# A two-layer graph net on one core: all projections in pairs of seven half products, y first, then layer 0

## The chip, the core and the metric

The kernel runs on one core of one Trainium2 chip. The time of a run is the device time in microseconds; lower is better. The core has five engines with an instruction queue each: TensorE (PE, matmuls; its weight loads are listed as PEld), VectorE (DVE), ScalarE (ACT), GpSimd (POOL) and SyncE (SP, which here only issues DMAs). Each engine works through its own queue in the order that was fixed when the program was built, and waits on semaphores of the others.

## What is computed

There are N = 2708 rows of D = 1024 float32 numbers and an adjacency matrix of zeros and ones with 10,979 ones. The reference, cut to what matters:

```python
# layer 0
q = x @ W_q.T + b_q;  k = x @ W_k.T + b_k;  v = x @ W_v.T + b_v
z = (q @ k.T) / sqrt(1024) * adj
z = where(z == 0, -10000, z)
x1 = layernorm(x + relu(softmax(z, axis=1) @ v))
# layer 1
out = layernorm(x1 + adj @ (x1 @ weight) + bias)
```

A row without neighbours has only masked scores, so its softmax is even over all rows and its layer-0 sum is the mean of all rows of v. 178 rows are of this kind.

## The kernel before

The kernel uses that the matrix is sparse. Rows are sorted by their number of neighbours and cut into 22 blocks of 128 (the last has 20 rows). `SLOTS` gives for each block how many neighbours its rows may have; block 0 holds the rows with most neighbours and is treated in shares, "hub" among them. Blocks 0 to 7 are the first family, 8 to 21 the second. A flag, computed on the chip, sends inputs that don't fit to a dense fallback, which this input doesn't use.

The score of rows i and j is x_i M x_j plus a term in j and i alone, with M = Wq^T Wk. So the kernel works in these stages:

- **0 to 138 us.** The weights are loaded and turned, M is made (L627, 256 matmuls, copied by ScalarE into `m_sb`), and VectorE and ScalarE look for the ones of the adjacency matrix, one block of columns at a time (`list_columns`, L235).
- **y, 138 to about 520 us.** `y_block` makes y = xM + bias for a block: 16 matmuls of 128 rows against 512 columns (L336), two accumulators, two additions by VectorE into one of two buffers `yo` (L340), and a store to y_d in DRAM. `column_sums` adds the columns of x on ScalarE meanwhile (L349), and `load_x` fetches a later block of x^T into one of three buffers. The 14 y blocks of the second family are woven together with the attention of the first.
- **Layer 0.** For each block GpSimd gathers the rows of y (L360) and the neighbours' rows of x (L366) by indirect DMA, VectorE forms the scores (L831) and, after the softmax, the weighted sum r (L888, L965). Then r is turned by TensorE (16 transposes, L734) and copied by ScalarE (L735), multiplied by Wv^T, finished on VectorE (bias, relu, residual) and ScalarE (layer norm), and scattered to x1_d (L721).
- **Layer 1, from about 747 us.** The neighbours' x1 rows are gathered and added (L1256, L1259), turned, multiplied by w1, normed and scattered to the output, in "units" of two blocks; the first unit is block 20 alone.

The product by Wv exists in two forms. `project` does one block in 16 matmuls (L757): blocks 6, 5, 4, 3, 2, 1, 0 take it, as "v" steps between y blocks or behind them. `pair_products` does two blocks at once. It cuts both turned blocks and the weight into halves, and takes seven half products of four matmuls (L1017) in place of eight. For that it needs four sums S of the turned halves (`turn_pair`, L1006 to L1009, VectorE) and differences of the weight's quarters (made once, L1154 and its neighbours), and each accumulator is read by VectorE more than once (`add`, L1029): seven reads for a pair. Seven pairs of layer 0, and ten units of layer 1, take this form. `project_mean` handles the last block, all of whose rows have the same sum.

The order is made by a planner at build time. `steps` is a list of products in order: y blocks, "v" steps, then pairs. `jobs` is a list of attention pieces. Each step adds a credit of TensorE time (`STEP`, 14.7, or twice that for a pair), each job takes its estimated VectorE time off (`SLOT`, `SMALL`), and jobs are emitted while credit is left and while fewer sums r are alive than there are buffers (`RB`). A scheduler then orders each queue; evictions have a high priority (`URGENT`).

```python
for h in range(NH):
    po = p_o.tile([P, HALF], F32, name="po")
    for c in range(DC):
        put = nc.tensor.matmul(po, xt[:, c, :], m_sb[c // 2][:, c % 2, k0:k1], ...)
    nc.vector.tensor_add(yo[:n, k0:k1], po[:n], y_bc[:n, k0:k1])
```

Of the kernel before, what the change touches and what calls it, by code (L numbers as in the profile page):

```python
# [31 lines left out]
SLOTS = [15, 11, 8, 6, 5, 4, 3, 2] + [13, 5, 4, 4, 3, 3, 3, 2, 2, 2, 1, 1, 1, 0]  # L32
ALONE = [8]
# [5 lines left out]
EARLY = 15  # L39
G1 = 9  # L40
RB = 3
# [39 lines left out]
def sparse_part(ctx, tc, x, xT, adj, wqT, wkT, wvT, bq, bk, bv, w1, b1, out):  # L81
# [29 lines left out]
    with es:  # L111
# [88 lines left out]
        loaded, sorted_, products, applied = [], [], [], []  # L200
# [88 lines left out]
        def load_x():  # L289
            b = len(xts)  # L290
            if b == NB:
                return
            r0, n = b * P, rows[b]
            xt = xa.tile([P, DC, P], F32, name="xt", bufs=3)
            if n < P:
                nc.gpsimd.memset(xt, 0.0)
            nc.sync.dma_start(out=xt[:, :, :n], in_=xT[:, r0:r0 + n].rearrange("(c p) n -> p c n", p=P))
            xts.append(xt)

        load_adj()  # L300
        load_x()
        load_x()
        load_x()
        yos = [xa.tile([P, YW], F32, name=f"yo{k}", bufs=1) for k in range(2)]
        def y_block(b):
            r0, n = b * P, rows[b]
            xt = xts[b]
            if b == NB - 1:
                column_sums(b)

                nc.vector.tensor_reduce(xbT, xs, AX.X, ALU.add)
                nc.vector.tensor_scalar_mul(xbT, xbT, 1.0 / N)
            yo = yos[b % 2]
            y_d, o0 = y_ds[b >= FAMILY], r0 - FAMILY * P * (b >= FAMILY)
            if b == NB - 1:

                assert n <= HUB
                po = p_o.tile([P, HALF], F32, name="po")
                with tc.high_priority(URGENT):
                    for c in range(DC):  # L320
                        for g in range(G):
                            nc.tensor.matmul(po[g * HUB:(g + 1) * HUB, :YW // G], xt[:, c, :HUB],
                                             m_sb[c // 2][:, c % 2, g * YW // G:(g + 1) * YW // G], start=(c == 0), stop=(c == DC - 1))
                    for g in range(G):
                        gs, cs = slice(g * HUB, g * HUB + n), slice(g * YW // G, (g + 1) * YW // G)
                        nc.vector.tensor_add(yo[gs, cs], po[gs, :YW // G], y_bc[gs, cs])
                for g in range(G):
                    gs, cs = slice(g * HUB, g * HUB + n), slice(g * YW // G, (g + 1) * YW // G)
                    nc.sync.dma_start(out=y_d[o0:o0 + n, cs], in_=yo[gs, cs])
                return  # L330
            firsts = []
            for h in range(NH):
                k0, k1 = h * HALF, (h + 1) * HALF
                po = p_o.tile([P, HALF], F32, name="po")
                for c in range(DC):
                    put = nc.tensor.matmul(po, xt[:, c, :], m_sb[c // 2][:, c % 2, k0:k1], start=(c == 0), stop=(c == DC - 1))  # L336
                    if c % (DC // 2) == 0:
                        firsts.append(put)
                with tc.high_priority(URGENT):
                    nc.vector.tensor_add(yo[:n, k0:k1], po[:n], y_bc[:n, k0:k1])  # L340
            products.append(put)
            if b < NB - 1:
                column_sums(b, firsts)
            load_x()
            nc.sync.dma_start(out=y_d[o0:o0 + n, :D], in_=yo[:n, :D])
# [257 lines left out]
        def records_back(f, behind=None):  # L603
            b0, nb = families[f]
            bs, js = slice(b0, b0 + nb), slice(0, max(SLOTS[max(b0, 1):b0 + nb]))
            if f == 0:
                deg0 = lists.tile([P, 1], F32, name="deg0")
                follow(nc.vector.tensor_copy(deg0, tab0[:, DEG:DEG + 1]), products[-1])
                nc.vector.tensor_scalar_add(deg0[:HUB], deg0[:HUB], float(-J0))
                masks(valid0, less0, deg0)  # L610
# [6 lines left out]
        m_sb = [wm_pool.tile([P, 2, YW], F32, name=f"m_sb{q}", tag=f"m{q}") for q in range(4)]  # L617
        for q in range(4):
            nc.vector.memset(m_sb[q][:, :, D:], 0.0)
            nc.vector.tensor_copy(m_sb[q][:, :, D], u_col[:, 2 * q:2 * q + 2])  # L620
        done = 0
        for i in range(DC):
            for h in range(NH):
# [5 lines left out]
                nc.scalar.copy(m_sb[i // 2][:, i % 2, hs], po)  # L629
# [5 lines left out]
                if not sorted_ and done > FAMILY + 2:  # L635
                    sort_end(0)
                    sorted_.append(0)
        y_bc = xa.tile([P, YW], F32, name="y_bc", bufs=1)
# [10 lines left out]
        for b in range(FAMILY):  # L649
            while done < min(NB, EARLY + 2 * (b + 1)):  # L650
                list_columns()
                done += 1
            y_block(b)
            if b in (0, 1, 3, 4, 5, 6):
                next(deal)
            if b == FAMILY - DC // 2 - 3:
                wv_q = quarters_of("wv")
            elif FAMILY - DC // 2 - 2 <= b < FAMILY - 2:
                for c in range(2 * (b - FAMILY + DC // 2 + 2), 2 * (b - FAMILY + DC // 2 + 2) + 2):
                    for h in range(NH):  # L660
                        put = nc.sync.dma_start(out=wv_q[c // 4][h][:, c % 4, :],
                                                in_=wvT[c * P:(c + 1) * P, h * HALF:(h + 1) * HALF])
                        follow(put, products[-2])
            if b == FAMILY - 4:
                sort_begin(1)
            if b == FAMILY - 3:
                sort_end(1)
            if b == 0:
                records_back(0)
# [23 lines left out]
        c_all = stat.tile([P, NB - 1, YW - D], F32, name="c_all", bufs=1)  # L693
        nc.vector.memset(c_all, 0.0)
        def row_constants(f):
            b0, end = families[f][0], min(sum(families[f]), NB - 1)
            for b in range(b0, end):
                xg = g_tile()
                nc.sync.dma_start(out=xg, in_=x[b * P:(b + 1) * P])
                nc.vector.scalar_tensor_tensor(junkv, xg, 1.0, u_bc, op0=ALU.mult, op1=ALU.mult, accum_out=c_all[:, b, 0:1])  # L700
            put = nc.vector.tensor_scalar(c_all[:, b0:end, 0], c_all[:, b0:end, 0], y_bc[:, D:D + 1], None, op0=ALU.add)
            nc.sync.dma_start(out=y_ds[f][:(end - b0) * P, D:].rearrange("(b p) e -> p b e", p=P), in_=c_all[:, b0:end])
            return put

        put = row_constants(0)
        records_back(1, put)

# [3 lines left out]
        def gather_x(src, b):  # L711

            xr = wp.tile([P, D], F32, name="xr", bufs=3)
# [38 lines left out]
        def project(rT, w):  # L752
            po = []
            for h in range(NH):
                acc = p_o.tile([P, HALF], F32, name="po")
                for c in range(DC):
                    put = nc.tensor.matmul(acc, rT[:, c, :], w[c // 4][h][:, c % 4, :],  # L757
                                           start=(c == 0), stop=(c == DC - 1))
                po.append(acc)
            products.append(put)  # L760
            return po

        def project_mean(rT, w):

            acc = p_o.tile([P, HALF], F32, name="po")
            with tc.high_priority(URGENT):
                for c in range(DC):
                    for g in range(G):
                        k = g % 2 * D // G
                        nc.tensor.matmul(acc[g * HUB:(g + 1) * HUB, :D // G], rT[:, c, :],  # L770
                                         w[c // 4][g // 2][:, c % 4, k:k + D // G], start=(c == 0), stop=(c == DC - 1))
# [3 lines left out]
            for h in range(NH):  # L775
                acc = p_o.tile([P, HALF], F32, name="po")
                for g in range(h * G // NH, (h + 1) * G // NH):
                    k = g * D // G - h * HALF
                    put = nc.tensor.matmul(acc[:HUB, k:k + D // G], ident[:, g * HUB:(g + 1) * HUB], quarters,
# [65 lines left out]
        def attend(b, got):  # L845
# [4 lines left out]
            for i, (j0, j1) in enumerate(cut):  # L850
# [33 lines left out]
                else:  # L884
                    r = xb_pools[0].tile([P, D], F32, name="r") if b in ALONE else wp.tile([P, D], F32, name="r", bufs=RB)
# [7 lines left out]

        def mean_rows(b):
# [4 lines left out]
            r = wp.tile([P, D], F32, name="r", bufs=RB)  # L899
# [18 lines left out]
        def finish0(b, po, xr):  # L918
            n = rows[b]
            t = xb_pools[0].tile([P, D], F32, name="t", bufs=3) if b in [0] + last else wp.tile([P, D], F32, name="t")  # L920
# [10 lines left out]
        def attend_shares(b, got):  # L931
# [4 lines left out]
            else:  # L936
                J, tab, far_less, rec, to, far, top = J0, tab0, less0, tab0, to_0, far_0, top2[:, 1:2]
                r = wp.tile([P, D], F32, name="r", bufs=RB)
# [56 lines left out]
        def turn_pair(flips, pool):  # L995

            A = []
            for k, flip_to in enumerate(flips):
                rT = (pool if k else wp).tile([P, DC, P], F32, name="rT", bufs=2)
                A.append(flip_to(rT))  # L1000
            if len(flips) == 1:
                return A, None
# [3 lines left out]
            nc.vector.tensor_add(S[0], a21, a22)  # L1006
            nc.vector.tensor_sub(S[1], S[0], a11)
            nc.vector.tensor_sub(S[2], a11, a21)
            halves_turned.append(nc.vector.tensor_sub(S[3], a12, S[1]))  # L1009
# [5 lines left out]
        def half_products(acc, a, w, start=True, stop=True):  # L1015
            for k in range(DC // 2):
                put = nc.tensor.matmul(acc, a[:, k], w[:, k], start=start and k == 0, stop=stop and k == DC // 2 - 1,  # L1017
# [644 lines left out]
```

## Time and profile before

| | |
|---|---|
| median of three runs | 1067.79 us (1062.9 to 1069.05) |
| the profiled execution | 1068.97 us, its span on the core 1067.1 us |
| mean granted TensorE clock | 0.983 |
| DMA | 229.25 MB, mean 215 GB/s |
| L757, single products by Wv | 97.8 us in 224 records |
| L734, transposes | 43.0 us in 320 records |
| L627, product M | 110.5 us in 256 matmuls, 40 to 138 us |

The times in the page are from one profiled execution. "Busy" is the time in which an engine works on an instruction that isn't a wait, a branch or a DMA issue. A group's row gives the line, the engine, what is written and read with their shapes, the count of records, their busy time and mean duration, and then the idle time just before them with the instruction that ended most of it. A float32 matmul leaves two records. Of the chain of waits that ended last, TensorE holds 23% of the span in the part that could be followed back:

```profile
PE 23%; DVE 11%; issue 6%; DMA 5%; POOL 4%; ACT 1%; POOLq 0%; DVEq 0%
```

The first y block starts in a gap: TensorE begins it at 138.40, stands still for 4.08 us until ScalarE has copied a part of the bias row `y_bc`, and goes on at 145.30. VectorE is then still busy with column lists, and comes to the first addition of y at 159.41.

### The profile page before, as it was taken

Reading aid. Unit: us, or ns where it says so; the run is one execution under the profiler, and the core shown is the slowest. Engines: PE = TensorE matmul, PEld = TensorE weight load, DVE = VectorE, ACT = ScalarE, POOL = GpSimd, SP = SyncE. Lnnn points to the kernel's source line nnn. Section 1 sums busy time; section 2 is a strip of 40 time slices with the busy share of each in tenths; the row PEclk is TensorE's granted clock in tenths of the full one; section 3 lists DMA queues with packets and bytes.
Section 4 is the critical chain, followed back from the end, with each engine's and each line's share of the span. In section 5 each row is a group of like instructions: output and inputs, shape, how many; then the busy total and the mean of one; then the engine's idle time right before and its main releaser. Section 6 shows DMA issues by size and latency. Waiting matters only on the chain.

```text
span 1067.1 us, 10904 instructions
## 1 busy us (share of the span) xinstructions
PE 1007.6 (94%) x2849; PEld 475.4 (45%) x2849; DVE 813.5 (76%) x2021; ACT 426.5 (40%) x894; POOL 494.0 (46%) x534
## 2 busy tenths in 40 slices
PE   7999989999998999999999999999589999999993
PEld 6444444444443444444544444444334444454441
DVE  8999789435387879999399999965677876987432
ACT  4599994222032332224424344332323363333321
POOL 0000350046454445526157666511677777887300
PEclk9999999999999999999999999999789999999997
DMA  9688867534777656796443778726689589979701
GB/s 349 214 285 255 254 184 256 160 116 119 269 262 234 223 172 207 224 346 192 162 127 94 243 241 267 253 80 229 162 278 264 179 276 318 293 210 321 191 40 42
DMA packets 106288, 229.25 MB, mean 215 GB/s; under 512 B 22898, under 2 KB 50298, under 8 KB 106216
## 3 DMA queue, kind: packets, MB, share of 16 engines
q0 software_dynamic: 48768, 148.05, 43.8%
q1 hardware_dynamic: 57448, 80.42, 23.3%
q8 instruction: 24, 0.39, 0.1%
q14 instruction: 48, 0.39, 0.1%
HBM read 219.61 MB, written 33.68 MB: 237 GB/s over the span
## 4 chain that ended last, share of the span: by engine, by line
PE 23%; DVE 11%; issue 6%; DMA 5%; POOL 4%; ACT 1%; POOLq 0%; DVEq 0%
PE po L1017 20%; DMA g<-x_d,tabs 3%; DVE r L888 3%; DVE junkv L831 2%; POOL g L366 1%; PE po L757 1%; DVE t L1029 1%; POOL xr L360 1%; DMA yg<-y_d,tabs 1%; PE tr L734 1%; DVE r L1259 1%; PE tr L747 1%; ACT junks L793 1%; DVE t L1087 1%; POOL r L366 0%
## 5 line engine op out<-in xcount | busy, mean ns | idle before, releaser
L336 PE MATMUL po<-m_sb,xt 128*128 128x512 f32 x672 | 293.7, 596 | 5.5 <-DVE yo L340 5.5
L336 PEld LDWEIGHTS po<-m_sb,xt 128*128 128x128 f32 x672 | 127.0, 191 | 163.4 <-issue 153.4
L831 DVE SCALAR_TENSOR_TENSOR junkv<-yg,g 128x1024 uint8<-128x1024 f32 x109 | 132.8, 1219 | 41.2 <-DMA yg<-y_d,tabs 20.0
L366 POOL DMA_INDIRECT g<-in_x_dram,tabs x86 | 112.1, 1304 | 70.6 <-DVE r L888 21.1
L1017 PE MATMUL po<-t,s_all 128*128 128x512 f32 x272 | 125.9, 606 | 4.7 <-DVE xr L1029 4.7
L1259 DVE SCALAR_TENSOR_TENSOR r<-g,valid,r 128x1024 f32<-128x1024 f32 x77 | 98.6, 1281 | 19.5 <-DMA g<-x_d,tabs 18.8
L627 PE MATMUL po<-wk_o,wq_o 128*128 128x512 f32 x256 | 110.5, 592 | 0.0
L757 PE MATMUL po<-wv,rT 128*128 128x512 f32 x224 | 97.8, 594 | 2.6 <-ACT junka L349 2.1
L793 ACT ACTIVATE junks<-t,lnm 128x1024 uint8<-128x1024 f32 (+1 forms) x41 | 47.0, 1147 | 125.6 <-DVE lnm L791 95.4
L349 ACT ACTIVATE junka<-xt 128x128 f32<-128x128 f32 x176 | 54.1, 307 | 91.9 <-PE po L336 69.6
L366 POOL DMA_INDIRECT g<-x_d,tabs x67 | 79.5, 1186 | 22.7 <-issue 14.0
L1017 PE MATMUL po<-w,rT 128*128 128x512 f32 x192 | 86.4, 599 | 0.0
L888 DVE SCALAR_TENSOR_TENSOR r<-g,pr,r 128x1024 f32<-128x1024 f32 x64 | 81.8, 1279 | 5.2 <-ACT r L900 4.6
L1017 PEld LDWEIGHTS po<-t,s_all 128*128 128x128 f32 x272 | 52.3, 194 | 71.8 <-issue 61.7
L235 DVE FIND_INDEX8 at_a<-ones,a 128x8 uint16<-128x83 f32 (+3 forms) x132 | 82.5, 631 | 0.6 <-issue 0.6
L806 ACT ACTIVATE t<-t,nmr,rstd 128x1024 f32<-128x1024 f32 (+1 forms) x41 | 50.0, 1237 | 81.3 <-DVE nmr L805 74.7
L627 PEld LDWEIGHTS po<-wk_o,wq_o 128*128 128x128 f32 x256 | 48.3, 190 | 59.3 <-issue 58.4
L1017 PE MATMUL po<-w,s_all 128*128 128x512 f32 x160 | 72.1, 592 | 0.0
L757 PEld LDWEIGHTS po<-wv,rT 128*128 128x128 f32 x224 | 42.2, 190 | 55.5 <-issue 51.4
L735 ACT COPY rT<-tr 128x512 f32<-128x512 f32 x80 | 43.1, 585 | 55.3 <-PE tr L734 55.2
L1017 PE MATMUL po<-t,rT 128*128 128x512 f32 x136 | 61.1, 592 | 0.0
L734 PE MATMUL tr<-ident,r 128*128 128x128 f32 x320 | 43.0, 281 | 18.1 <-DVE r L1256 12.2
(356 smaller groups left out, 1466.3 us busy)
## 6 DMA issues: line engine op xcount, KB each, us to landing
xt<-in_xT_dram SPq DMA_DIRECT2D x21, 512.0 KB, 6.3
g<-in_x_dram SPq DMA_DIRECT2D x21, 512.0 KB, 7.7
y_d<-yo SPq DMA_DIRECT2D x21, 512.0 KB, 6.3
a<-in_adj_dram SPq DMA_DIRECT2D x21, 413.5 KB, 5.2
a<-in_adj_dram SPq DMA_DIRECT2D x21, 338.5 KB, 4.5
a<-in_adj_dram SPq DMA_DIRECT2D x21, 263.5 KB, 5.2
wq_i<-in_wqT_dram SPq DMA_DIRECT2D x8, 512.0 KB, 5.9
wk_i<-in_wkT_dram SPq DMA_DIRECT2D x8, 512.0 KB, 11.0
```

The lines of the kernel that those rows point to most:

```text
L235: nc.vector.max_index(at[:n, i], ones[:n, :8], a[:n, cuts[i] + 8 * i:cuts[i + 1] + 8 * i + 8])
L336: put = nc.tensor.matmul(po, xt[:, c, :], m_sb[c // 2][:, c % 2, k0:k1], start=(c == 0), stop=(c == DC - 1))
L349: put = nc.scalar.activation(junka, xts[b][:, c, :], AF.Copy, accum_out=xs[:, c, b:b + 1])
L366: nc.gpsimd.indirect_dma_start(out=dst[:n], out_offset=None, in_=src, in_offset=bass.IndirectOffsetOnAxis(ap=at, axis=0), bounds_check=N - ...
L627: nc.tensor.matmul(po, wq_o[i // 2][:, o, i % 2 * P:(i % 2 + 1) * P], wk_o[:, o, hs], start=(o == 0), stop=(o == DC - 1))
L734: nc.tensor.transpose(tr[:, k, :], r[:, c * P:(c + 1) * P], ident)
L757: put = nc.tensor.matmul(acc, rT[:, c, :], w[c // 4][h][:, c % 4, :], start=(c == 0), stop=(c == DC - 1))
L793: nc.scalar.activation(junks[:n], t[:n], AF.Square, bias=nm[:n], accum_out=vs[:n])
L831: nc.vector.scalar_tensor_tensor(junkv[:n], yg[:n, :D], scale, xg[:n], op0=ALU.mult, op1=ALU.mult, accum_out=s)
L888: nc.vector.scalar_tensor_tensor(r[:n], xg[j][:n], pr[:n, j:j + 1], r[:n], op0=ALU.mult, op1=ALU.add)
L1017: put = nc.tensor.matmul(acc, a[:, k], w[:, k], start=start and k == 0, stop=stop and k == DC // 2 - 1, skip_group_check=True)
L1259: put = nc.vector.scalar_tensor_tensor(r[:n], xg[:n], ok[:n, j:j + 1], r[:n], op0=ALU.mult, op1=ALU.add)
```

## The change

Four things change.

1. y. All of y but the last two blocks is made in pairs by `pair_products`: ten pairs, then block 20 alone (`y_single`), then the short block 21 in small matmuls on parts of the array (`y_last`). M is kept as four quarters `m_q` whose differences are formed in place and in three more tiles `m_t`, on VectorE, while M is made; these tiles, and the sums `y_s`, stand where the weights wv were. The sums S of a pair of y are formed by GpSimd. The buffers for x^T go from three to four and those for y from two to three, one list of columns more is done ahead of y, and the weights wv are loaded only after the last pair of y.
2. Layer 0. `project` and the "v" steps are gone. All y steps come first, then ten pairs, with the mean rows as a step after the first pair. The first family's weighted sums stay in their buffers until then: `RB` goes from 3 to 5, and the first two lie in the buffers of `t`. The sums S of these pairs too are formed by GpSimd, not VectorE (`turn_pair` has a new argument for the engine); in layer 1 VectorE keeps them. The planner's constants are new, and residual rows `xr` have two buffers for three.
3. Block 20 loses its only slot (`SLOTS`), since none of its rows has a neighbour. It becomes a second block of mean rows in both layers, without gather, score, sum and transposes.
4. Layer 1 begins with the pair (19, 18) in place of the unit (20,).

The core of the diff:

```diff
-SLOTS = [15, 11, 8, 6, 5, 4, 3, 2] + [13, 5, 4, 4, 3, 3, 3, 2, 2, 2, 1, 1, 1, 0]
-ALONE = [8]
+SLOTS = [15, 11, 8, 6, 5, 4, 3, 2] + [13, 5, 4, 4, 3, 3, 3, 2, 2, 2, 1, 1, 0, 0]
+FIRST = [6, 5]
-EARLY = 15
+EARLY = 16
-RB = 3
+RB = 5
-            xt = xa.tile([P, DC, P], F32, name="xt", bufs=3)
+            xt = xa.tile([P, DC, P], F32, name="xt", bufs=4)
-        yos = [xa.tile([P, YW], F32, name=f"yo{k}", bufs=1) for k in range(2)]
+        yos = [xa.tile([P, D], F32, name=f"yo{k}", bufs=1) for k in range(3)]
...
+        def y_pair(b):
+            xp = [xts[b], xts[b + 1]]
+            (a11, a12), (a21, a22) = [halves_of_turned(x_) for x_ in xp]
+            S = [y_s[:, i] for i in range(4)]
+            nc.gpsimd.tensor_tensor(S[0], a21, a22, op=ALU.add)
+            nc.gpsimd.tensor_tensor(S[1], S[0], a11, op=ALU.subtract)
+            nc.gpsimd.tensor_tensor(S[2], a11, a21, op=ALU.subtract)
+            nc.gpsimd.tensor_tensor(S[3], a12, S[1], op=ALU.subtract)
...
+            pair_products(xp, S, m_q, m_t, [base, base], to, whole)
...
+                if i < DC // 2:
+                    nc.vector.tensor_sub(t1[:, k], t1[:, k], w11[:, k])
+                else:
+                    nc.vector.tensor_sub(m_t[0][:, k], w22[:, k], t1[:, k])
+                    nc.vector.tensor_sub(m_t[1][:, k], m_t[0][:, k], w11[:, k])
+        nc.vector.tensor_sub(m_t[2], m_q[1][0], m_t[0])
...
-        def turn_pair(flips, pool):
+        def turn_pair(flips, pool, engine):
...
-            nc.vector.tensor_add(S[0], a21, a22)
+            engine.tensor_tensor(S[0], a21, a22, op=ALU.add)
...
-        STEP, Y_END, P_END, END, SLOT, SMALL = 14.7, 2.8, 5.0, 3.3, 2.6, 1.5
+        PAIR, EVICT, FLIP, END, SLOT, SMALL = 24.3, 4.8, 2.2, 2.6, 2.6, 1.5
-        pairs = [(7, 20), (19, 18), (17, 8), (16, 11), (15, 10), (9, 14), (13, 12)]
+        pairs = [(6, 5), (4, 3), (2, 1), (0, 7), (19, 18), (17, 8), (16, 11), (15, 10), (9, 14), (13, 12)]
-        steps = [("y", 8), ("y", 9), ("y", 10), ("y", 11), ("y", 12), ("v", 6), ("y", 13), ("v", 5), ("y", 14), ("v", 4), ("y", 15), ("v", 3),
-                 ("y", 16), ("v", 2), ("y", 17), ("y", 18), ("y", 19), ("y", 20), ("y", 21)]
-        steps += [("v", b) for b in [1, 0] + last] + [("p", pair) for pair in pairs]
+        steps = [("y", b) for b in list(range(FAMILY, NB - 2, 2)) + [NB - 2, NB - 1]]
+        steps += [("p", pairs[0]), ("mean", tuple(last))] + [("p", pair) for pair in pairs[1:]]
...
+                if b == NB - 2:
+                    wv_q = quarters_of("wv")
+                    for j in range(NH):
+                        for k in range(2):
+                            for c in range(DC // 2):
+                                r0 = k * HALF + c * P
+                                nc.sync.dma_start(out=wv_q[k][j][:, c, :], in_=wvT[r0:r0 + P, j * HALF:(j + 1) * HALF])
+                    y_single(b)
...
-        units = [(20,), (19, 18), (17, 16), (15, 1), (14, 2), (7, 8), (9, 3), (4, 10), (6, 0), (5, 11), (12, 13)]
+        units = [(19, 18), (17, 16), (15, 1), (14, 2), (7, 8), (9, 3), (4, 10), (6, 0), (5, 11), (12, 13)]
```

## The prediction

> **What bounds the kernel now.** I read the page first: busy shares, then the 40 slices.
>
> ```profile
> span 1067.1 us, 10904 instructions
> PE 1007.6 (94%) x2849; PEld 475.4 (45%) x2849; DVE 813.5 (76%) x2021; ACT 426.5 (40%) x894; POOL 494.0 (46%) x534
> ...
> PE   7999989999998999999999999999589999999993
> ...
> DVE  8999789435387879999399999965677876987432
> ...
> POOL 0000350046454445526157666511677777887300
> ```
>
> TensorE is busy for 1007.6 of 1067.1 us and idle for 59.5. Whatever takes matmuls away shortens the span, as long as nothing else comes to the end first. The row under it shows what could: VectorE has nines from slice 16 to slice 26. So next I read the busy time of each engine in stretches of 20 us (columns: stretch, its length, then busy time and instructions of PE, PEld, DVE, ACT, POOL, the granted clock, DMA share, GB/s).
>
> ```profile
> 260.00:280.00 20.00, 20.00 (x48) 8.82 (x47) 2.19 (x9) 2.41 (x12) 13.87 (x14) 1.00 0.83 286
> ...
> 460.00:480.00 20.00, 20.00 (x49) 8.94 (x48) 19.41 (x31) 3.22 (x16) 5.82 (x4) 1.00 0.96 354
> ...
> 580.00:600.00 20.00, 20.00 (x54) 9.28 (x53) 20.00 (x50) 7.79 (x17) 12.77 (x11) 1.00 0.69 211
> ...
> 620.00:640.00 20.00, 19.91 (x53) 9.11 (x52) 19.89 (x47) 8.64 (x17) 13.77 (x12) 1.00 0.73 243
> ```
>
> At 260 VectorE has nothing to do; from 420 to 500 and from 540 to 700 it is as full as TensorE. Over all stretches from 240 to 740, which hold y of the second family and layer 0, its busy times add up to 405.6 of 500 us. Two engines are bounds in turn, and the change takes from one of them. The groups give the prices:
>
> ```profile
> L336 PE MATMUL po<-m_sb,xt 128*128 128x512 f32 x672 | 293.7, 596 | 5.5 <-DVE yo L340 5.5
> L831 DVE SCALAR_TENSOR_TENSOR junkv<-yg,g 128x1024 uint8<-128x1024 f32 x109 | 132.8, 1219 | 41.2 <-DMA yg<-y_d,tabs 20.0 <-DMA g<-in_x_dram,tabs 17.1 <-DMA g<-in_x_dram,tab_h 2.0
> ...
> L1017 PE MATMUL po<-t,s_all 128*128 128x512 f32 x272 | 125.9, 606 | 4.7 <-DVE xr L1029 4.7
> ```
>
> and, with different shapes kept apart, two rows of VectorE:
>
> ```profile
> L340 DVE TENSOR_TENSOR yo<-po,y_bc 128x512 f32<-128x512 f32 x42 | 28.3, 682 | 26.1 <-PE po L336 14.8 <-DMA y_d<-yo 5.7 <-DMA wv<-in_wvT_dram 5.6
> ...
> L1006 DVE TENSOR_TENSOR s_all<-rT 128x512 f32<-128x512 f32 x17 | 11.7, 686 | 0.0
> ```
>
> L336 has 32 records for each of 21 blocks (a float32 matmul is recorded twice), so a block costs 293.7/21 = 14.0 us in 16 matmuls, 0.874 us each. The means of single records overlap and aren't summed.
>
> **What the Trainium skill says.** "SBUF — State Buffer", section "Who interferes with whom": a VectorE instruction with two SBUF inputs contends with a GpSimd instruction that reads SBUF; the shared port pair is an exclusive lock, so the later one waits for the whole instruction. The trace of before can't confirm it: its GpSimd instructions are nearly all DMA issues, and the score at L831, two SBUF inputs, keeps 1219 ns throughout. "GPSIMD Engine Reference", section "3.1 Elementwise — side-by-side cycle accounting": a float32 tensor_tensor of 2048 elements takes 4497 ns there against 2293 on VectorE. The VectorE figure agrees with this trace (2287 ns for the one 128x2048 subtraction, L1154); GpSimd's no row shows. Scaled to 512 elements it gives an estimate of 4497/4 = 1.12 us, or 1.24 with a fixed 156 ns that doesn't shrink. I take 1.24.
>
> **The change part by part, TensorE first.**
>
> 1. y in pairs. Seven half products of four matmuls are 28 × 0.874 = 24.5 us, two single blocks 28.0: 3.5 us less in each of 10 pairs, −35.0. The short last block has 40 small matmuls for 32: some 3.7 us become 4.6, +0.9. Sum −34.1.
> 2. Layer 0 without single blocks. The seven at L757 cost 97.8 us; three more pairs cost 73.4. Sum −24.4.
> 3. Block 20 without a slot. Its single unit at the head of layer 1 goes (16 matmuls, −14.0) and its transposes in both layers (L734: 43.0 us / 20 flips = 2.15, twice, −4.3). A second mean row adds about 0.9.
>
> Sum −34.1 − 24.4 − 14.0 − 4.3 + 0.9 = −75.9. With unchanged idle time the span is 991.2.
>
> **What VectorE pays and saves from 240 to 740.** Sums S of layer 0 move off it: 7 pairs × 4 × 0.68 = −19. A pair of y needs seven evictions instead of four: six pairs here, 18 × 0.68 = +12. Three more pairs in place of seven singles: 21 evictions plus 6 residual adds for 14 and 7 long ones, and 3 more differences elsewhere, +8 by my count. Block 20's score, sum and norm −3. It stays at about 404 us. TensorE's part of the same stage is 6 × 24.5 + 14.0 + 4.6 = 165.6 for y and 10 × (24.5 + 4.3) + 5 = 293 for layer 0, 459 together. VectorE is thus 88% loaded where it was 81%. In the built program's order, with the durations of this trace, VectorE has 23 to 25 us of work between the evictions of one y pair and of the next, against 24.5 on TensorE: next to no slack there, some 2 to 4 us in each layer-0 pair. Of the waits at L831 (37 us on gathers) most can shrink, since a busier engine comes later to its data.
>
> **GpSimd.** 80 sums at 1.24 us are 99 us of new work, 4 to 5 us a pair, with 5 to 14 of 20 us used per stretch: it fits. But all gathers are issued in the same queue, and the order shows sums that wait for TensorE (S is one buffer in y) or for ScalarE's copies ahead of gathers. A pair's third half product needs S[1], 7 us after the pair starts, and S[1] of the pair before is free long ahead; the gathers behind wait a few us. Cost between 0 and 2 us a pair, taken with the next item.
>
> **The shared port.** 64 of the sums lie in the stage where VectorE is near full. About 245 of its 405 us there are scores and weighted sums with two SBUF inputs, 60%. Lower end: nothing. Upper end: every sum stops VectorE in full, 64 × 1.24 = 79 us, of which 55 (459 − 404) would be covered if the slack lay in the right places; it doesn't in y. I take 2 to 3 us lost in each of six y pairs and nothing in layer 0's: about +14.
>
> **Smaller terms.**
> - Start of y. VectorE is 97% full from 40 to 120 us with the column lists, and its first eviction at L340 starts at 159.41. The change puts 12 subtractions of 0.69 and one of 2.29 (10.6 us) ahead of it and takes two lists of some 5.2 us out. So the first eviction stays near 159, but the first accumulator is wanted at about 153: +6, from 0 to 10. TensorE's wait of 4.08 us for ScalarE at 141 stays.
> - Coupling within pairs: accumulators are reused, so each eviction must come within 3.5 us. In 17 pairs of before this cost 4.7 us at the matmuls and 8.2 at their weight loads, 0.76 a pair; 13 more pairs, +10.
> - The weights wv. In before their loads lie in family 1 and y loses some 7 us from 280 to 340 (5.6 at L340). Now they need the tiles of m's differences and S, so they are issued after the last y pair, in SP's queue between y stores, 4 MB in all. At 354 GB/s, the rate from 460 to 480, this is 12 us; 14.0 + 4.6 us of single y covers it in part. Lost 5 to 10; net of the gain, +1, from −7 to +10.
> - Head of layer 1: a pair now stands where a single unit was, and needs its differences and sums first. Between −5 and +5, taken at nothing.
> - Longer life of family 1's sums (five buffers and two more), three x blocks for residuals turned into two, three y buffers for two, list columns moved: hidden by queues that have slack; if not, they show as waits inside the stage above.
>
> Sum: 991.2 + 14 + 6 + 10 + 1 = 1022 less 4 for the idle of L336 in old y (5.5 us, at L340), which the pairs replace: 1018. The profiled execution took 1068.97 for a span of 1067.1, 1.9 more, and lies 1.2 above the median of the runs (1067.79). So 1020.
>
> **Rivals.**
> - R1, the cover holds: the port costs nothing, gathers come in time, pair coupling is the only new stall. Span about 998, time 1000. For it: 88% load. Against: the twenties of VectorE from 560 to 640, and no slack within y pairs.
> - R2, the port locks in full where VectorE is full: +42 for 14 (some 5 us in six y pairs, 1 in ten others). Time 1046. For it: the skill's rule. Against: GpSimd as the later one may be the one that waits.
> - R3, slower: VectorE becomes the bound from the second family to the end of layer 0. Its 404 us, the 37 of waits for gathers that stay because GpSimd issues late behind its sums, and 64 sums at a price L each: past 459 + 68 = 527 us the change loses (991 + 17 of small terms + 68 = 1076, 0.5% more than before in time). That is at L = (527 − 441)/64 = 1.34 us a sum, lock and late gathers together. An operation that takes 2 us on GpSimd, half more than my estimate, and locks, gives 569 us and a time near 1118. Against: all of the lock, and the whole of the old idle time on top, must come together.
> - R4, nothing: the same with L about 1.2, within 0.5% (5.3 us, about what a measurement of this kernel can tell from no change). That the change doesn't do what it says I exclude: the order of the built program has 28 long matmuls to a pair and the sums on GpSimd.
>
> **How the numbers follow.** Forecast 1020 with its own range 1003 to 1037: 0.50. R1: 0.12. R2, 1037 to 1062: 0.16. R4: 0.07. R3: 0.15. Faster is 0.50 + 0.12 + 0.16 = 0.78. The range from 994 to 1071 leaves out the lower quarter of R1 and nearly all of R3, 0.18 or so.
>
> **What would show it.** Right: TensorE's busy time near 932 us; y's stage some 34 us shorter; sums on GpSimd of 1.1 to 1.3 us; VectorE in the nineties through y of family 2; a gap of about 6 us in TensorE near 153; idle time of TensorE between 70 and 95 us. The port shows as scores longer than 1219 ns while a sum runs. R1: such scores unchanged and idle near 65. R3: TensorE's idle time over 140 us in y of family 2 and layer 0, released by VectorE's evictions, with sums of 2 us or more. The forecast is wrong if the matmuls of a pair cost other than 24.5 us, or if the wv loads stop TensorE for over 15 us.

## The result and the profile after

The changed kernel takes 1150.28 us, the median of four runs (1138.66 to 1154.56), against 1067.6 before; the ratio is 1.0765, with a 95% interval from 1.068 to 1.0851. It is 83 us slower. The forecast was 1020.

The page of the changed kernel, the rows that answer to those of before:

```profile
span 1147.9 us, 10767 instructions
PE 973.5 (85%) x2697; PEld 458.3 (40%) x2697; DVE 882.4 (77%) x2041; ACT 426.8 (37%) x893; POOL 602.1 (52%) x610
...
PE   7999868994698898769988889899599894999994
...
DVE  8899799642598999789989999964469774696532
...
PEclk9999978997699899979999899999799997998997
```

TensorE has 152 records fewer, as the change intends, but its idle time went from 59.5 to 174.4 us, and it is busy for 973.5 us where the forecast's sum left 1007.6 − 75.9 = 931.7. VectorE, which was to stay as it was, is busy for 69 us more. GpSimd's 108 us more come from the 80 sums, which take some 117:

```profile
L913 DVE SCALAR_TENSOR_TENSOR junkv<-yg,g 128x1024 uint8<-128x1024 f32 x108 | 151.2, 1400 | 26.3 <-DMA yg<-y_d,tabs 13.0 <-DMA g<-in_x_dram,tabs 5.8 <-DMA g<-in_x_dram,tab 5.4
...
L970 DVE SCALAR_TENSOR_TENSOR r<-g,pr,r 128x1024 f32<-128x1024 f32 x64 | 91.3, 1427 | 1.4 <-ACT r L968 1.2
...
L306 PE MATMUL po<-mt,y_s 128*128 128x512 f32 x160 | 82.7, 665 | 41.9 <-DVE yo L320 41.9
...
L320 DVE TENSOR_TENSOR yo<-po,y_bc 128x512 f32<-128x512 f32 x42 | 28.7, 683 | 16.9 <-PE po L306 16.9
...
L372 POOL TENSOR_TENSOR y_s<-y_s,xt 128x512 f32<-128x512 f32 x10 | 16.5, 1651 | 0.5
...
L371 POOL TENSOR_TENSOR y_s<-xt 128x512 f32<-128x512 f32 x10 | 13.3, 1328 | 49.5 <-PE po L306 49.4
```

Scores went from 1219 to 1400 ns and weighted sums from 1279 to 1427; the evictions, which read one operand from an accumulator and one from SBUF, stayed at 683. The last row shows something else: the first of y's four sums waits 49.4 us in all until TensorE has done with the buffer, and what stands behind it in GpSimd's queue, gathers too, waits as well.

The stretches between four marks say where the time went. The marks are the first y matmul, the first score, the first gather of layer 1 and the end (columns as before: stretch, length, PE, PEld, DVE, ACT, POOL, clock, DMA share, GB/s). The kernel before:

```profile
138.40:285.71 147.31, 143.23 (x343) 64.10 (x342) 83.19 (x300) 52.81 (x167) 50.61 (x77) 0.99 0.59 191
285.71:755.62 469.91, 449.52 (x1309) 208.71 (x1307) 398.41 (x791) 163.38 (x450) 226.56 (x166) 0.99 0.63 205
755.62:1067.10 311.48, 283.06 (x784) 134.95 (x784) 208.91 (x366) 100.40 (x172) 197.44 (x153) 0.95 0.71 217
```

The changed kernel:

```profile
147.47:308.74 161.27, 124.77 (x276) 54.61 (x276) 101.25 (x306) 52.64 (x171) 72.96 (x81) 0.87 0.43 137
308.74:824.85 516.11, 440.69 (x1256) 204.55 (x1256) 446.75 (x805) 158.28 (x437) 307.64 (x223) 0.95 0.60 196
824.85:1147.90 323.05, 274.59 (x744) 129.92 (x744) 204.93 (x360) 103.91 (x176) 197.10 (x152) 0.92 0.69 209
```

Of the 80.8 us between the spans, 9.1 come before y, 14.0 before the first score, 46.2 between the first score and layer 1, and 11.6 in layer 1. Every stage is longer, those in which TensorE has less to do too.

How a stop looks on TensorE (start, duration, instruction and count, in brackets the idle time before it and what ended it):

```profile
162.35 6.34 PE L306 MATMUL po<-mt,y_s 128*128 128x512 f32 x8 [6.19 <-DVE yo L320]
168.53 3.60 PE L306 MATMUL po<-m,y_s 128*128 128x512 f32 x8
...
292.45 6.14 PE L306 MATMUL po<-mt,y_s 128*128 128x512 f32 x8 [21.33 <-DVE yo L320]
...
357.02 3.67 PE L306 MATMUL po<-mt,y_s 128*128 128x512 f32 x8 [3.54 <-DVE yo L320]
...
386.96 6.68 PE L306 MATMUL po<-mt,y_s 128*128 128x512 f32 x8 [2.79 <-DVE yo L320]
```

Eight records are one half product. It takes 3.60 us, and the next one starts 3.43 us after it. Behind a stop of 5 us or more y's half products take 5.5 to 6.3 us: each long stop is paid twice. The Trainium skill gives the cause ("TensorE: Matmul & The Clock Gate", section "What's actually happening": the array drops to half clock after an idle window of about 3.4 us). For the long stops this trace agrees. For shorter ones the length alone doesn't decide it: the half product behind a stop of 3.54 us took 3.67 us, the one behind 2.79 us took 6.68. The mean granted clock is 0.931 for 0.983. By the two traces' records of the granted clock, TensorE works 76.8 us at half clock, against 14.6 in the kernel before. Half of that, 38 and 7 us, is time lost.

### The profile page after: what moved, and what is told of

The parts are those of the page before. It is cut to its first block, busy times and chain, and to the rows that moved or that the text cites. A ratio compares the mean times of both kernels' runs of the same rounds, so it can differ in the third digit from the quotient of the medians.

```text
span 1147.9 us, 10767 instructions
## 1 busy us (share of the span) xinstructions
PE 973.5 (85%) x2697; PEld 458.3 (40%) x2697; DVE 882.4 (77%) x2041; ACT 426.8 (37%) x893; POOL 602.1 (52%) x610
## 4 chain that ended last, share of the span: by engine, by line
DVE 25%; PE 23%; issue 15%; POOL 10%; DMA 10%; ACT 1%; SPq 0%; POOLq 0%; DVEq 0%; ACTq 0%
PE po L306 22%; DVE junkv L913 5%; DVE r L970 4%; DMA g<-x_d,tabs 3%; POOL g L458 3%; POOL xr L452 2%; DMA g<-in_x_dram,tabs 2%; DVE t L320 2%; DVE junkv L796 2%; DVE r L1054 1%; DVE yo L320 1%; POOL tab_d L673 1%; DMA xr<-x_d,tabs 1%; DVE r L1314 1%; DVE t L1118 1%
## 5 line engine op out<-in xcount | busy, mean ns | idle before, releaser
L913 DVE SCALAR_TENSOR_TENSOR junkv<-yg,g 128x1024 uint8<-128x1024 f32 x108 | 151.2, 1400 | 26.3 <-DMA yg<-y_d,tabs 13.0
L306 PE MATMUL po<-t,s_all 128*128 128x512 f32 x320 | 152.5, 621 | 18.7 <-DVE xr L320 7.5
L458 POOL DMA_INDIRECT g<-in_x_dram,tabs x84 | 113.9, 1356 | 51.1 <-issue 13.8
L306 PE MATMUL po<-mt,y_s 128*128 128x512 f32 x160 | 82.7, 665 | 41.9 <-DVE yo L320 41.9
L306 PEld LDWEIGHTS po<-t,s_all 128*128 128x128 f32 x320 | 62.6, 199 | 103.1 <-issue 89.4
L970 DVE SCALAR_TENSOR_TENSOR r<-g,pr,r 128x1024 f32<-128x1024 f32 x64 | 91.3, 1427 | 1.4 <-ACT r L968 1.2
L306 PE MATMUL po<-w,rT 128*128 128x512 f32 x160 | 75.9, 616 | 15.1 <-DVE t L1351 15.1
L306 PE MATMUL po<-m,xt 128*128 128x512 f32 x192 | 86.4, 603 | 0.0
L306 PE MATMUL po<-m,y_s 128*128 128x512 f32 x160 | 73.8, 605 | 5.4 <-DVE yo L320 5.4
L306 PE MATMUL po<-wv,rT 128*128 128x512 f32 x160 | 76.5, 628 | 0.0
L306 PE MATMUL po<-t,rT 128*128 128x512 f32 x160 | 74.3, 607 | 1.6 <-DVE t L320 1.6
L306 PE MATMUL po<-wv,s_all 128*128 128x512 f32 x160 | 72.8, 593 | 0.7 <-DVE t L320 0.7
L832 PE MATMUL tr<-ident,r 128*128 128x128 f32 x304 | 44.7, 295 | 32.3 <-DVE r L1311 13.9
```

The source lines that it names most:

```text
L458: nc.gpsimd.indirect_dma_start(out=dst[:n], out_offset=None, in_=src, in_offset=bass.IndirectOffsetOnAxis(ap=at, axis=0), bounds_check=N - ...
L832: nc.tensor.transpose(tr[:, k, :], r[:, c * P:(c + 1) * P], ident)
L913: nc.vector.scalar_tensor_tensor(junkv[:n], yg[:n, :D], scale, xg[:n], op0=ALU.mult, op1=ALU.mult, accum_out=s)
L970: nc.vector.scalar_tensor_tensor(r[:n], xg[j][:n], pr[:n, j:j + 1], r[:n], op0=ALU.mult, op1=ALU.add)
```

## The experiments

Two theories stood at first. P: the sums on GpSimd hold VectorE up through the shared port. Q: VectorE's queue stands still in a few places in front of an eviction that a pair waits for. The kernel before was timed again beside each group of runs; its median stayed between 1066.5 and 1068.2.

**The sums on VectorE (s_dve).**

```diff
-            nc.gpsimd.tensor_tensor(S[0], a21, a22, op=ALU.add)
+            nc.vector.tensor_tensor(S[0], a21, a22, op=ALU.add)
...
-turn_pair([flip_of(b_) for b_ in c], xb_pools[0], nc.gpsimd)
+turn_pair([flip_of(b_) for b_ in c], xb_pools[0], nc.vector)
```

> All 80 sums S of y and layer 0 on VectorE in place of GpSimd. Theory P: scores go back from 1400 to 1219 ns and weighted sums from 1427 to 1279, some 45 us of VectorE time back against 54 us of sums added; gathers come earlier, so the time falls, to about 1120 to 1135. Theory Q: VectorE's queue gets no shorter (54 added, 45 returned), the gaps at 292, 494, 830 and 964 stay; time 1145 to 1175.

1090.36 us, ratio 1.0217 (1.0186 to 1.0248): 60 us back, more than either theory said. Theory Q's four stops are still there (18.2, 9.2, 13.8 and 13.5 us), for 21.3, 12.5, 13.9 and 15.1, so most of the 60 us came from elsewhere.

```profile
PE 956.8 (88%) x2697; PEld 454.0 (42%) x2697; DVE 863.1 (80%) x2121; ACT 430.2 (40%) x893; POOL 491.3 (45%) x530
...
L913 DVE SCALAR_TENSOR_TENSOR junkv<-yg,g 128x1024 uint8<-128x1024 f32 x108 | 131.2, 1215 | 10.3 <-DMA yg<-y_d,tabs 9.2 <-DMA g<-in_x_dram,tabs 0.6 <-DMA g<-in_x_dram,tab 0.4
```

VectorE does 80 sums of 0.68 us more, 54.4 us, and is busy for 19.3 us less. So the sums on GpSimd had made its other work 73.7 us longer, 0.92 us a sum, and scores are back at 1215 ns. But this run moves two things at once. The sums leave the shared port, and they leave GpSimd's queue, where they stood ahead of gathers: VectorE's idle time at the scores, nearly all of it for gathers, is 10.3 us here and was 26.3. How the 60 us divide between the two isn't shown.

**That part alone in the kernel before (before_s_pool).** `turn_pair` gets the engine as an argument, and the 28 sums of layer 0 go to GpSimd.

```diff
-            nc.vector.tensor_add(S[0], a21, a22)
+            engine.tensor_tensor(S[0], a21, a22, op=ALU.add)
...
-... for b_ in c], xb_pools[0])
+... for b_ in c], xb_pools[0], nc.gpsimd)
```

> The kernel before with one part of the change alone: the 28 sums S of layer 0's seven pairs on GpSimd, layer 1 unchanged. Theory P (each sum takes VectorE about 0.9 us where the two meet, as the 74 us of longer VectorE instructions for 80 sums say): VectorE gets 19 us rid and 26 us longer, and scores in 580 to 700 go from 1219 to about 1400 ns; since both engines are full there, the time rises by 5 to 25 us, to 1073 to 1093. Rival (the sums alone are harmless, it is the pairs of y that can't stand them): 1064 to 1071.

1090.95 us, ratio 1.0222 (1.0179 to 1.0264). VectorE is rid of 19.1 us of sums and yet busy for 6.4 more: 25.5 us longer, 0.91 a sum. Its busy times, and a piece of its timeline that shows why:

```profile
PE 1016.5 (93%) x2849; PEld 478.5 (44%) x2849; DVE 819.9 (75%) x1993; ACT 424.3 (39%) x894; POOL 531.8 (49%) x562
...
595.72 1.28 POOL L1006 TENSOR_TENSOR s_all<-rT 128x512 f32<-128x512 f32 x1
595.79 4.75 DVE L831 SCALAR_TENSOR_TENSOR junkv<-yg,g 128x1024 uint8<-128x1024 f32 x1
596.95 1.28 POOL L1008 TENSOR_TENSOR s_all<-rT 128x512 f32<-128x512 f32 x1
598.17 1.27 POOL L1007 TENSOR_TENSOR s_all<-s_all,rT 128x512 f32<-128x512 f32 x1
```

A score that takes 1.22 us alone takes 4.75: it waits for three whole sums. That is the lock that the Trainium skill names ("SBUF — State Buffer", section "Who interferes with whom"). Late gathers can explain little here, since the idle time at the scores is 45.2 us for 41.2. So most of the 24 us that this run loses is the price of the port, in a schedule that is otherwise the old one.

**y without pairs (y_single, y_single_s_dve, y_plain).** In the first, `y_pair` calls `y_single` twice. The second also keeps layer 0's sums on VectorE. The third, besides, drops M's differences and reads each accumulator once, when whole:

```diff
-            half_products(pa, a1, w11, stop=False)
-            add(to[1], pa, base[1])
-            half_products(pb, a1, t1, stop=False)
-            half_products(pb, a2, w22, start=False)
-            add(to[1], pb, to[1])
-            products.append(half_products(pa, a2, w21, start=False))
-            add(to[0], pa, base[0])
+            half_products(pa, a1, w11, stop=False)
+            half_products(pa, a2, w21, start=False)
+            add(to[0], pa, base[0])
+            half_products(pb, a1, t1, stop=False)
+            products.append(half_products(pb, a2, w22, start=False))
+            add(to[1], pb, base[1])
```

> All y in single blocks of 16 matmuls, the rest as changed; no sums S in y. TensorE works 35 us more. Theory Q: a single block's accumulators can wait longer for VectorE, so most of the 62 us of gaps between 147 and 460 and the slow half products behind them (some 20 us) go; the time falls to 1100 to 1120. Rival (VectorE is the bound in this stage whatever form y has): the gaps go, but the time stays, 1140 to 1160. If the gaps were not due to pairs: 1175 to 1185.

> Like s_dve, but y in single blocks; TensorE works 35 us more and VectorE 27 us of sums less. If pairs of y are worth their 3.5 us each once the shared port is out of the way, this is slower than s_dve: 1105 to 1125. If the accumulators' coupling eats the gain (gaps of about 31 us in s_dve from 147 to 320, slow halves behind them), it is 1080 to 1095.

> Like y_single_s_dve (1114.8), but the single blocks of y have no read in mid-chain, as in the kernel before: two accumulators of eight matmuls each, read once when whole, and no differences of M. Same 16 matmuls a block. Theory K (what stops TensorE in y is that an accumulator must be read by VectorE in mid-chain, within 3.5 us, however long VectorE's queue stands): the gaps of 5.6, 13.3, 7.9, 2.5 and 5.5 us between 194 and 371 and the slow halves behind them go, and 10 us of VectorE work at the start; 1070 to 1085. Rival (VectorE's waits for the hub's gathers and for y stop TensorE in any form): gaps stay over 20 us in sum, 1100 to 1115.

They take 1143.17, 1114.8 and 1110.43 us. The first two differ by layer 0's 40 sums alone: 28 us. Against s_dve the single blocks lose 24 and the plain ones 20: with the port free, pairs of y are worth most of their 35 us. Theory K had the gaps mostly right and the time wrong. In y_plain the stop of 13.3 us is gone, but TensorE then stands 16.2 us at 497 for the mean of x, which VectorE comes to late. From the first accumulator to there, TensorE's stops of over 2 us add up to 43 us in y_single_s_dve and to 34 in y_plain: without reads in mid-chain most of the standing is still there, the longest stop now at the end of the stage.

**The stop at 292 (hub_first, hub_early, hub_late).** In the changed kernel VectorE stands before a row of the hub's tables, ahead of the evictions in its queue:

```profile
257.43 0.69 DVE L320 TENSOR_TENSOR yo<-po,yo 128x512 f32<-128x512 f32 x1 [2.74 <-PE po L306]
278.81 2.14 DVE L594 TENSOR_SCALAR valid_h<-found 128x11 f32<-128x11 f32 x1 [20.69 <-DMA found<-keys_d,at_i]
```

GpSimd issues the eleven gathers of found behind fourteen scatters, 1.27 us each. Three kernels move that. hub_first is the changed kernel with the gathers ahead; the others start from s_dve, hub_early with the hub's fourth stage a pair earlier, hub_late with L594 behind the pair's last eviction:

```diff
             elif q == 2:
-                sort_end(1)
                 next(deal)
+                sort_end(1)
```

```diff
             elif q == 1:
+                next(deal)
                 sort_begin(1)
             elif q == 2:
                 sort_end(1)
-                next(deal)
```

```diff
-            nc.vector.tensor_scalar(valid_h, found, 0.0, None, op0=ALU.is_gt)
+            follow(nc.vector.tensor_scalar(valid_h, found, 0.0, None, op0=ALU.is_gt), added[-1], same=True)
```

> The eleven gathers of found are issued ahead of the fourteen scatters to tab_d. Theory Q (the loss sits in a few places where VectorE's queue stands still in front of an eviction that a pair's accumulator waits for): TensorE's gap of 21.3 us at 292 shrinks to about 7 us, and the slow half product behind it goes with it; the time falls by 14 to 20 us, to about 1132. Theory P (the GpSimd sums hold VectorE up through the shared port, everywhere): the gap moves but the time stays within 5 us of 1150.

> Like s_dve (1090), with the hub's fourth stage (its positions and records) one pair of y earlier; the gathers of found are then issued some 25 us earlier. Theory Q: the gap of 18.2 us at 285 goes to under 5; the wait for yg behind it, which the first score needs, stays, so 8 to 14 us fall: 1076 to 1082. Rival (VectorE only waits elsewhere, as in all_mended, where 6 and 13 us replaced 18): 1087 to 1093.

> Like s_dve (1090), with the first VectorE row that waits for the hub's gathers put behind the last eviction of the fourth pair of y instead of in its midst. Theory Q (in a pair, TensorE is stopped by what VectorE's queue waits for ahead of a mid-chain eviction): the gap of 18.2 us at 285 shrinks to 0 to 6 us and the slow half behind it goes; TensorE is then some 15 us ahead at the first score, which the stage behind it can use as far as VectorE (426 of 465 us busy there) lets it: 1074 to 1084. Rival (VectorE bounds that stage from the first score on): the gap goes and the time stays, 1087 to 1093.

1142.61, 1094.65 and 1095.71 us: 8 us less than the changed kernel, and 4 and 5 more than s_dve, none of it far outside the spread. The stop of 21.3 us is gone in hub_first, but stops of 6.3 at 263, 4.7 at 284 and 9.5 at 309 stand in its place. The stop of 18.2 us of s_dve shrank to 11.3 in hub_late, with one of 8.5 behind it, and became 20.1 in hub_early. From the first score to layer 1 it is 465.0 us in s_dve, 466.2 in hub_late and 477.4 in hub_early:

```profile
302.08:767.09 465.01, 425.59 (x1248) 201.13 (x1248) 426.06 (x863) 160.65 (x433) 224.14 (x164) 0.97 0.66 216
```

This is s_dve. TensorE's head start isn't used there. In the three kernels VectorE works 424 to 430 us in that stretch and TensorE 418 to 433. Each is idle for some 39 to 48 us, so neither fills the stretch alone, and what sets its length isn't shown.

**The weights wv (wv_behind).** From s_dve, the three differences of wv that wait for TensorE's last use of M's tiles are put behind the last evictions of y:

```diff
-                nc.vector.tensor_sub(wv_t[0], q22, q12)
+                put = nc.vector.tensor_sub(wv_t[0], q22, q12)
+                for tail in tails:
+                    follow(put, tail, same=True)
```

> Like s_dve (1090), and the three differences of wv that wait for TensorE are put behind the last evictions of y and the mean of x in VectorE's queue. Theory Q: the gap of 9.2 us at 460 shrinks to under 3, time 1078 to 1084. Rival (the differences are then late for the first pair of layer 0, which gives the gain back): 1087 to 1092.

1099.64 us, 9 more than s_dve. The stop at 460 went from 9.2 to 6.9, and stops of 4.4 at 477 and 4.6 at 560 came in. TensorE's stops of over 2 us from 455 to 560 add up to 20 us in both kernels, so the gain is given back there, as the rival said. The time lies outside the rival's range too, and the 9 us more stay unexplained.

**Layer 1 (mean_apart, before_no20, l1_no_hub, apart_no_hub).** The changed kernel has a stop of 15.1 us at 964. Two blocks of mean rows share two buffers xr with the next unit, so gather, norm, store and the next gather follow one another:

```profile
945.78 2.10 POOL L452 DMA_INDIRECT xr<-x_d,tabs  x1 [0.31 <-issue]
...
953.97 1.01 POOL L819 DMA_INDIRECT out_dram<-xr,tabs  x1 [3.45 <-ACT xr L888]
958.92 1.04 ACT L1324 COPY xr<-bias 20x1024 f32<-20x1024 f32 x1 [5.23 <-DMA out_dram<-xr,tabs]
...
963.95 2.07 PE L306 MATMUL po<-w,rT 128*128 128x512 f32 x2 [15.09 <-DVE t L1351]
```

mean_apart finishes them three units apart, l1_no_hub leaves out the hub's gathers and sums of layer 1 (from s_dve), apart_no_hub does both (from s_dve), and before_no20 is the kernel before without the unit of block 20:

```diff
-            if i == 2:
-                for b in last:
-                    pending.append((b, gather_x1(b), None))
+            if i in (2, 5):
+                b = last[i // 3]
+                pending.append((b, gather_x1(b), None))
```

```diff
-                sum_rows("hub")
+                pass
```

```diff
-        units = [(20,), (19, 18), (17, 16), (15, 1), ...
+        units = [(19, 18), (17, 16), (15, 1), ...
```

> In layer 1 the two blocks of mean rows are finished three units apart and not together. Theory Q: with two buffers xr, three residuals in a row wait for each other's gather, norm and scatter; taken apart, the gap of 15.1 us at 964 goes, and with it part of the slow clock behind it: 1128 to 1135. Rival (two buffers are too few anyway, or layer 1 is bound by its gathers): less than 5 us gained.

> The kernel before without the unit of block 20 in layer 1 (its gather, transposes, products, norm and store are left out, so block 20 of the output isn't written). TensorE has 16 us less to do there. Theory G (layer 1 is bound by the queue of GpSimd's gathers, not by TensorE): the time falls by what three or four GpSimd issues cost, 0 to 6 us, to 1061 to 1067. If layer 1 is bound by TensorE: 14 to 16 us less, 1051 to 1054.

> Like s_dve (1090), with the hub's eleven gathers and sums of layer 1 left out (the hub rows of the output lack that part). TensorE's work is the same. Theory G: eleven issues of about 1.5 us each go from GpSimd's queue, 12 to 17 us less, 1073 to 1078. If TensorE is the bound of layer 1: within 3 us of 1090.

> Like s_dve (1090), with the mean rows of layer 1 apart and the hub's gathers and sums of layer 1 left out (the hub rows of the output lack that part). Theory G2 (two limits of layer 1 stand in line, the ring of two residual buffers and then GpSimd's queue, so that taking one alone shows nothing): layer 1, 316.8 us in s_dve from its first gather to the end, becomes 295 to 305; time 1070 to 1079. If something else bounds it (the first gathers' latency and the tail on TensorE): 1086 to 1092.

mean_apart: 1146.05 us; the stop at 964 is gone, and stops of 6.0 at 1030 (for the hub's sums: VectorE forms five of them without a pause up to that moment) and 3.1 at 1054 stand in its place. before_no20: 1069.09, ratio 1.0007 (0.9982 to 1.0032): some 15 us of matmuls and transposes out of layer 1 change nothing, TensorE's busy time there falls by 10 us, and layer 1 takes 311.6 us for 311.5. l1_no_hub: 1090.56, no change. apart_no_hub: 1071.73, 19 us less than s_dve, and layer 1 takes 296.5 us:

```profile
772.99:1069.50 296.51, 266.73 (x744) 126.36 (x744) 193.33 (x349) 102.43 (x176) 181.87 (x141) 0.96 0.70 212
```

Two limits stand in line: the ring of residual buffers, and behind it the hub's part. Taking one alone brings about 4 us, not clear of the spread, or nothing; taking both brings 19. That the second limit is GpSimd's queue of gathers, as theory G2 has it, isn't shown: with the hub's eleven gathers go eleven sums of 1.28 us on VectorE, and the stop at 1030 in mean_apart ends with such sums.

**The parts together (all_mended, hub_late_apart).** all_mended joins s_dve, hub_first, wv_behind and mean_apart; hub_late_apart joins hub_late and mean_apart.

> Sums on VectorE, the hub's gathers ahead of the scatters, wv's differences behind the last evictions, the mean rows of layer 1 apart. If the parts add up (60, 7, 8 and 4 us of 1150): about 1071, within 1% of the kernel before. If the gap at 285 (18 us) goes in full, 1060. If layer 1 is bound by its gathers, the last part brings nothing: 1075.

> hub_late and the mean rows of layer 1 apart, nothing left out: the best that the runs so far suggest. If both parts count: 1068 to 1080. Against the kernel before (1067.8) I expect no gain over it.

1090.16 and 1091.31 us. Neither differs from s_dve: the parts don't add up, though all_mended also holds wv_behind, which alone lost 9 us. No version that computes everything beats the kernel before.

## Why the prediction was wrong

The step that failed is the sentence "With unchanged idle time the span is 991.2", with the terms put on top of it. TensorE was to be idle for 70 to 95 us and was idle for 174.4, and its work at half clock was in no term. The points follow the terms of the sum.

1. **TensorE's work, −75.9: right in the main, some 71 by the records.** 168 records of 128x512 went, at 0.43 us each, −72. But L734's 320 records are 40 flips of eight transposes, not 20 (the kernel's description has sixteen for a block; they are for two), so two flips less are −2.15 and not −4.3; and the small products of the short block and of the mean rows cost 3.4 us more in all, not 1.8. What failed is that less work makes a shorter span. before_no20 shows it for layer 1, where some 15 us less bought nothing. In s_dve the stretch from first score to layer 1 shrank by 5 us, although TensorE was busy for 24 us less in it. TensorE was 94% busy, but it wasn't alone on the path.
2. **The shared port, +14: the term most mis-sized.** Taking the sums off GpSimd gave 60 us back (s_dve), late gathers included. What failed is "2 to 3 us lost in each of six y pairs and nothing in layer 0's": layer 0's sums alone cost 24 us in the old kernel and 28 in the new one with single y blocks. VectorE's work grew by 0.92 us a sum, three quarters of the 1.24 that the upper end took in full, because sums come in runs and one score waits for several (up to 5.3 us for one). The price of a sum was near: 1.24 estimated, 1.27 to 1.28 undisturbed, 1.46 in the mean. Part of that is luck, since the fixed 156 ns in it is what the Trainium skill's "GPSIMD Engine Reference", section "3.1 Elementwise — side-by-side cycle accounting", gives for an instruction's dispatch on VectorE, not on GpSimd.
3. **R2 and R3.** R2's mechanism, the full lock, is what was seen, with a larger price than its 42. R3 was nearer than it looked. With a flip at 1.08 us TensorE needs 6 × 24.5 + 14.0 + 4.6 + 10 × (24.5 + 2.15) + 5 = 437 us in the stage from 240 to 740, not 459. VectorE's 404 and 64 sums at the measured 0.92 make 463, an estimate like the forecast's own. So the cover of 55 us was 33, and R3's limit of 1.34 us a sum becomes (437 + 68 − 441)/64 = 1.0, of which the lock alone took 0.92. (R3's 1076 is also 0.8% above before, not 0.5%.) But R3's signs didn't come: TensorE's idle time from the first score to layer 1 is 75 us, not over 140, and no sum has a mean of 2 us. VectorE works 447 of the 516 us there, so that it alone set the pace isn't shown.
4. **Start of y, +6: right as a stop** (6.19 us at 162), but a second followed at 195 (5.3). "TensorE's wait of 4.08 us for ScalarE at 141 stays" was wrong: it is 7.94 us, and y starts 9.1 us later.
5. **Coupling within pairs, +10: right mechanism, wrong size.** The four groups of y's half products idle 55.3 us for evictions. The 0.76 a pair came from pairs whose VectorE queue held no long waits for gathers.
6. **wv, +1: in its range, for another reason.** The stop is 12.5 us, less some 7 of before. It wasn't the loads, but a difference that waits 6.85 us for TensorE in front of the evictions and the mean of x.
7. **Head of layer 1, 0: near** (13.9 for 11.6 us). But two residual buffers were "hidden by queues that have slack"; they made the stop of 15.1 us, even if its removal alone gave 4 (not clear of the spread).
8. **Not in the sum at all: the slow clock behind stops.** It costs 38 us of TensorE time where the kernel before pays 7, so 31 of the 42 us by which TensorE's busy time exceeds the forecast's 931.7. Some 5 more are point 1's; the rest is open.

What stays open is the remaining distance of s_dve, 23 us by the medians. Its profiled execution was the fastest of four, and of its span 6.4 us more lie before y, 10.0 before the first score and 5.3 in layer 1, against −4.9 in between, 16.8 in all. No run shortened the chain of lists and tables ahead of the first score (VectorE, then GpSimd's scatters and gathers); that it sets those 10 us is argued, not shown.

## What to carry to other kernels

A busy share of 94% doesn't make an engine the bound: cut the span at the marks where one stage's results let the next begin, and ask for each stage which engine would be late if the first were free. Small elementwise work handed to GpSimd is charged in large part to VectorE's instructions with two SBUF operands (0.91 and 0.92 us a sum of 1.27), so don't book it as free while VectorE is near full. Whether it pays where VectorE idles or reads accumulators, no run here shows. When an accumulator is read in mid-chain, a wait ahead of that read in the reader's queue can stop TensorE; reading it only when whole took a part of the standing away (43 us became 34). Each stop of over 5 us cost some 2 to 3 us more at half clock.

## What the runs showed of the hardware

A 128x512 float32 tensor_tensor on GpSimd takes 1.27 to 1.28 us when nothing is in its way and up to 1.80 in the mean of a row (L1009 in before_s_pool) beside a busy VectorE: both sides wait. The VectorE addition of an accumulator and an SBUF operand (yo<-po,y_bc) isn't touched: its mean is 682 to 685 ns in all these runs. Small instructions are: a tensor_tensor of 128x22 elements, 0.17 us in the kernel before, took 1.23 us beside a sum and ended as the sum did.

```profile
337.54 2.13 POOL L372 TENSOR_TENSOR y_s<-y_s,xt 128x512 f32<-128x512 f32 x1
338.48 1.23 DVE L1263 TENSOR_TENSOR over<-degs,cap 128x22 f32<-128x22 f32 x1
```
